# A graph-attention layer in units of half the nodes: two PSUM banks of sums, copied out by ScalarE, and weight tiles of 1024 columns

## The chip, the cores and the metric

The kernel runs on one core of a Trainium2 chip. The metric is the device time of one execution in microseconds (us); less is better. Times of engines below come from one profiled execution.

## The reference

Two layers follow each other, on x of shape (8, 2048, 256) with one adjacency matrix of 2048 by 2048 for all eight batches.

```
# layer 0: attention over chunks of 256 keys, 4 heads of 64
scores = clip(q k^T / 8, -10, 10), -10 where adj == 0
attn   = softmax(scores within each chunk of 256 keys)
x      = layernorm(x + layernorm((sum over chunks of attn v) Wo^T + bo + x))
# layer 1: graph attention, 4 heads of 64
Wh     = x W
e[i,j] = leaky_relu(s_src[i] + s_dst[j], 0.2), -inf where adj == 0
alpha  = softmax(e over j)
x      = layernorm(x + elu(alpha Wh))
```

The exponential of a leaky relu is a maximum of two products, so the kernel forms the weight of layer 1 as max(row factor, column factor) times the adjacency bit; the rest of the column factor is multiplied into Wh once per batch (the tile `waug`, which has a column of ones, times the factor, for the divisor).

## The kernel before

The batches are processed one after the other, and the work of two batches is woven together: while layer 0 of batch b runs, layer 1 of batch b-1 runs beside it. The order of instructions on every engine is the order in which the program lists them; nothing is reordered.

**Layer 0.** A batch has 64 slots (`SLOTS`): 4 groups of 512 queries, 2 pairs of heads, 8 chunks of 256 keys. In slot s the program issues, in this order, the scores of slot s+1 (`scores`, L377 on TensorE, then the masked clip L388 on VectorE), the first head's product of slot s (`product`, L412, copied out of PSUM by ScalarE at L419), the exponentials of slot s+1 (`exps`, L400, ScalarE), one step of layer 1 of the batch before (`lower.step`), and the second head's product of slot s. Around this stand the output projection, the two norms and the projections of layer 1 (`Between`, by tables that name the slot of each step), and the final norm of the batch before that (`Closing`, with tables `CLOSING`, `CLOSING_ALONE` and `ENDING`). Between two batches there is a stretch without slots, written out as the list `order`, in which the next batch is projected.

**Layer 1.** The class `Layer1` works in units: a group of node tiles of 128 (the output rows) and a head. `BANKS = (6, 5, 5)` cuts the 16 node tiles in three groups, so a batch has 12 units, and each unit runs over the 16 tiles of neighbours: 192 tiles in all, `STEP` = 3 in each of the 64 slots. For a tile, `make` forms the weights e on VectorE (L731, 768 or 640 columns), and `use` multiplies them on TensorE (L751), two halves of 64 rows for each node tile, into the unit's sums `pa`, which are held in one PSUM bank (6 x 65 columns of 512). Every such product is two records in the profile. `make` runs `STEP` tiles ahead of `use`. The tiles e live in 4 buffers of the pool `ep`, the adjacency bits `et` in 3 buffers of 4 tiles each (`JG`), loaded two groups ahead, and the row factors `srow` in 2 buffers; all are loaded by SP's queue. The pool `psL` has two banks that its users take in turn: `pa` of layer 1, the mask pieces and one product in the first batch, and one projection per batch.

When a unit is complete, `close` finishes it in pieces, one piece at each later step (`rest`): the divisor and its reciprocal on VectorE (L774, L775, from PSUM), one scaling per node tile on ScalarE from PSUM to `hh` (L779), exponential and relu on ScalarE (L783, L785), and their combination into h1 on VectorE (L787). Meanwhile the next unit writes the other bank of `psL`.

**The ends.** In the last batch `lower.step` is left out of the last `LATE` = 14 slots, and these 14 steps stand in `order` instead, among the steps of the last projection. After it layer 1 of the last batch runs alone, three tiles to a slot, with the final norms of the last two batches beside it.

**The masks.** In the first batch the class `Masks` reads the adjacency in 48 pieces of 128 by 768 or 640, turns them on TensorE and writes clip bounds (`clipD`) and edge bits (`edgeD`, one array for each group of node tiles) to DRAM. The raw pieces `araw` use the pool `ep` as well.

Of the kernel before, what the change touches and what calls it, by code (L numbers as in the profile page):

```python
# [8 lines left out]
F32 = mybir.dt.float32  # L9
# [8 lines left out]
P = 128  # L18
# [4 lines left out]
def adj_resnorm_kernel(  # L23
# [34 lines left out]
    FAR = 100.0  # L58
    BANKS = (6, 5, 5)
    assert D == 64 and KC == HP and 2 * D == P and sum(BANKS) == NT  # L60

# [8 lines left out]
    WIDE = max(BANKS)  # L70
    JG = 4
    assert TILES == STEP * SLOTS and NT % JG == 0

    consts = ctx.enter_context(tc.tile_pool(name="consts", bufs=1))
    big = ctx.enter_context(tc.tile_pool(name="big", bufs=1))
    prp = ctx.enter_context(tc.tile_pool(name="prp", bufs=4))
    ep = ctx.enter_context(tc.tile_pool(name="ep", bufs=4))
    slabs = ctx.enter_context(tc.tile_pool(name="slabs", bufs=4))
    edges = ctx.enter_context(tc.tile_pool(name="edges", bufs=3))
    blocks = ctx.enter_context(tc.tile_pool(name="blocks", bufs=2))  # L80
    small = ctx.enter_context(tc.tile_pool(name="small", bufs=2))
    psA = ctx.enter_context(tc.tile_pool(name="psA", bufs=1, space=bass.MemoryType.PSUM))
    psC = ctx.enter_context(tc.tile_pool(name="psC", bufs=1, space=bass.MemoryType.PSUM))
    psL = ctx.enter_context(tc.tile_pool(name="psL", bufs=2, space=bass.MemoryType.PSUM))
    psM = ctx.enter_context(tc.tile_pool(name="psM", bufs=1, space=bass.MemoryType.PSUM))
# [13 lines left out]

    turn_of = [0]  # L100

    def two_banks(shape, name):

        turn_of[0] ^= 1
        return psA.tile(shape, F32, tag=f"psA{turn_of[0]}", name=name)


# [91 lines left out]
    class Masks:  # L199
# [3 lines left out]
        def __init__(self):  # L203
            self.pieces = [
                (QT * q + u, m) for q in range(NCH) for m in range(len(BANKS)) for u in range(QT)
            ]
            self.raw, self.bits, self.done = [], [], []
            self.next = 0

        def step(self):  # L210
            send()
            if self.next < len(self.pieces):
                t, m = self.pieces[self.next]
                n, j0 = BANKS[m], FIRST[m]
                araw = ep.tile([P, WIDE * P], I32, tag="e", name="araw")
                nc.sync.dma_start(
                    out=araw[:, : n * P], in_=adj[t * P : (t + 1) * P, j0 * P : (j0 + n) * P]
                )
                self.raw.append((t, m, araw))
                self.next += 1  # L220
            if self.bits:
                t, m, ab = self.bits.pop(0)
                self.turn(t, m, ab)
            if len(self.raw) > 2 or (self.raw and self.next == len(self.pieces)):
                t, m, araw = self.raw.pop(0)
                w = BANKS[m] * P
                ab = small.tile([P, WIDE * P], BF16, tag="hh", name="ab")
                nc.vector.tensor_scalar(ab[:, :w], araw[:, :w], 0, None, ALU.not_equal)
                self.bits.append((t, m, ab))
# [4 lines left out]
        def turn(self, t, m, ab):  # L234
            n, j0 = BANKS[m], FIRST[m]
            pm = psL.tile([P, WIDE, P], BF16, tag="psL", name="pm")
            for k in range(n):
                nc.tensor.transpose(pm[:, k, :], ab[:, k * P : (k + 1) * P], identb)
            clip = small.tile([P, WIDE, P], I8, tag="ee", name="clip")
            nc.vector.tensor_scalar(clip[:, :n], pm[:, :n], 2 * CLIP, -CLIP, ALU.mult, ALU.add)  # L240
            edge = small.tile([P, WIDE, P], U8, tag="hp", name="edge")
            nc.scalar.copy(edge[:, :n], pm[:, :n])
            q, u = t // QT, t % QT
            mi = max(k for k in range(len(BANKS)) if FIRST[k] <= t)
            at = (t - FIRST[mi]) * P

            def stores():
                nc.sync.dma_start(
                    out=clipD[q][:, j0 : j0 + n, u * P : (u + 1) * P], in_=clip[:, :n]
                )  # L250
                nc.sync.dma_start(out=edgeD[mi][:, j0 : j0 + n, at : at + P], in_=edge[:, :n])

            outgoing.append(stores)
# [44 lines left out]
    def project(b, g):  # L298
# [14 lines left out]
        def linear(dst, w, bias, apart=False):  # L313
            if apart:
                pps = [psL.tile([P, CH], F32, tag="psL", name="pp") for _ in range(KC)]
            else:
                pp = two_banks([P, KC, CH], "pp")
                pps = [pp[:, c, :] for c in range(KC)]
            for c in range(KC):
                for kc in range(KC):  # L320
                    nc.tensor.matmul(  # L321
                        pps[c],
                        lhsT=w[:, kc, c * P : (c + 1) * P],
                        rhs=st["xT"][:, kc, :],
                        start=(kc == 0),
                        stop=(kc == KC - 1),
                    )
            for c in range(KC):
                nc.scalar.activation(  # L329
                    dst[:, c, cols], pps[c], AF.Identity, bias=bias[:, c : c + 1]  # L330
                )
# [70 lines left out]
    def product(s, k, alone):  # L402
# [3 lines left out]

        pool, tag = (psL, "psL") if alone and k else (psC, "psC")
        pc = pool.tile([P, QT, D1], F32, tag=tag, name="pc")
        for i in range(QT):
# [277 lines left out]
    class Layer1:  # L687
        def __init__(self, b, gd, waug):
            self.b, self.gd, self.waug = b, gd, waug
            self.made = self.used = 0  # L690
            self.rows, self.edge, self.e = {}, {}, {}
            self.tail = []
            self.load_edge(0)
            self.load_edge(1)
            self.load_row(0)
# [22 lines left out]
        def make(self):  # L718
# [8 lines left out]
            if j % JG == 0:  # L727
                self.load_edge(k // JG + 2)
            w = BANKS[m] * P
# [12 lines left out]
        def use(self):  # L742
            k = self.used
            n, j = k // NT, k % NT
            m, h = UNITS[n]
            if j == 0:
                self.pa = psL.tile([P, CH], F32, tag="psL", name="pa")
            e = self.e.pop(k)
            for i in range(BANKS[m]):
                for z in range(2):  # L750
                    nc.tensor.matmul(  # L751
                        self.pa[z * D : (z + 1) * D, i * D1 : (i + 1) * D1],
                        lhsT=e[:, i * P + z * D : i * P + (z + 1) * D],
                        rhs=self.waug[:, j, h, :],
                        start=(j == 0 and i == 0),
                        stop=(j == NT - 1 and i == BANKS[m] - 1),
                        skip_group_check=True,
                    )
            self.used += 1
            if j == NT - 1:  # L760
                self.tail.append(self.close(n, self.pa))

# [4 lines left out]

        def close(self, u, pa):
            m, h = UNITS[u]
            n = BANKS[m]  # L770
            pav = pa[:, : n * D1].rearrange("p (k d) -> p k d", k=n)

            dn = small.tile([P, n, 1], F32, tag="dn", name="dn")
            nc.vector.tensor_scalar(dn, pav[:, :, D:D1], 1e-30, None, ALU.max)  # L774
            nc.vector.reciprocal(dn, dn)  # L775
            yield 1
            hh = small.tile([P, n, D], F32, tag="hh", name="hh")
            for k in range(n):
                nc.scalar.activation(hh[:, k, :], pav[:, k, :D], AF.Copy, scale=dn[:, k, :])  # L779
            yield 1  # L780

            ee = small.tile([P, n, D], F32, tag="ee", name="ee")
            nc.scalar.activation(ee, hh, AF.Exp)  # L783
            hp = small.tile([P, n, D], F32, tag="hp", name="hp")
            nc.scalar.activation(hp, hh, AF.Relu)  # L785
            yield 1
# [58 lines left out]
    for g in range(NCH):  # L845
# [44 lines left out]
    ENDING = {  # L890
        25: [(0, "load")],
        28: [(0, "add")],
        29: [(0, "stats")],
        31: [(0, "finish")],
        46: [(1, "load")],
        49: [(1, "add")],
        50: [(1, "stats")],
        52: [(1, "finish")],
        SLOTS - 1: [(2, "load"), (3, "load")],
# [3 lines left out]
    for b in range(B):  # L903
# [108 lines left out]
        if b + 1 < B:  # L1012
# [3 lines left out]
            order = [begin, *rest, l1, *rest, *first, lambda: before.values((2, 3))]  # L1016
            order += [*rest, ctx, *rest, k0]
            order += [steps[0], t1, steps[1], v0, steps[2], steps[3], l2, k1, steps[4], q0]
# [3 lines left out]
        else:  # L1022
# [4 lines left out]
            order += [steps[7], step, steps[8], step, steps[9], step, fs[0], step, fs[1], step, fs[2]]  # L1027
            order += [step, lambda: lower.rest(4)]
            assert sum(p is step for p in order) == LATE
# [10 lines left out]
    for s in range(SLOTS + 1):  # L1040
        send()
        if s < SLOTS:
            lower.step()
        else:
            lower.rest(4)
        closing.do(s)
# [44 lines left out]
```

## Time and profile before

| What | Value |
|---|---|
| Median of 3 runs | 3788.8 us (3786.09 to 3789.01) |
| The profiled execution | 3787.69 us, of it the span of the instructions 3785.9 us |
| TensorE busy | 3676.4 us, 97% of the span |
| VectorE busy | 3196.2 us, 84% |
| ScalarE busy | 1945.2 us, 51% |
| GpSimd busy | 1385.6 us, 37% |
| Weight tiles e (L731) | 512 of 128x768, mean 1023 ns; 1024 of 128x640, mean 886 ns |
| Layer-1 products (L751) | 32768 records, 1080.3 us busy |
| TensorE's granted clock, mean | 0.992 |

The page gives busy time of each engine, then the span in 40 slices with a digit for the busy tenths, then the groups of instructions with their means and with the idle time of the engine before them. A mean counts an instruction from its first to its last work; back to back, two of them overlap a little, so that the distance from start to start, which the timeline shows, is shorter. The waits name for each idle stretch of an engine what ended it.

### The profile page before, as it was taken

To read this page: it belongs to the slowest core of one execution; us is meant where nothing else is said; L and a number is where in the kernel's file an instruction comes from. 1 tells how busy PE (TensorE), PEld (TensorE's weight loads), DVE (VectorE), ACT (ScalarE), POOL (GpSimd) and SP (SyncE) were. 2 spreads that over 40 slices of the span, in tenths; PEclk is the share of its full clock that TensorE was granted. 3 is DMA by queue.
4 is the path that set the end of the run, shared out by engine and by line. 5 is a ranking of instruction groups with operands and counts; after the bars stand their busy time and mean duration, and the time that the engine had idled before them with its cause. 6 is when DMAs were issued, how large, how long until landed. Compare 5 with 4: busy or idle time off the path is not lost. (4 is left out here: it accounts for less than half of the span.)

```text
span 3785.9 us, 160213 instructions
## 1 busy us (share of the span) xinstructions
PE 3676.4 (97%) x72100; PEld 2747.1 (73%) x72100; DVE 3196.2 (84%) x4810; ACT 1945.2 (51%) x3601; POOL 1385.6 (37%) x1202
## 2 busy tenths in 40 slices
PE   9999999999999999999999999999999999999787
PEld 5656677776777777776777767777677777776676
DVE  5877599987999689995999959998699968998798
ACT  4666445545555555554555545555555555555221
POOL 1445234333434244332433424443344434434310
PEclk9999999999999999999999999999999999999999
DMA  6652334433343343333433434433333334333354
GB/s 163 152 116 69 76 100 105 105 77 113 110 105 100 85 123 102 97 99 85 137 95 94 105 98 125 105 100 81 113 110 102 102 87 123 97 103 81 97 152 120
DMA packets 756545, 398.50 MB, mean 105 GB/s; under 512 B 425744, under 2 KB 721040, under 8 KB 755856
## 3 DMA queue, kind: packets, MB, share of 16 engines
q1 hardware_dynamic: 705856, 354.54, 36.4%
q10 hardware_dynamic: 50000, 33.70, 2.8%
q8 instruction: 564, 9.24, 1.0%
q14 instruction: 125, 1.02, 0.1%
HBM read 331.22 MB, written 56.89 MB: 103 GB/s over the span
## 5 line engine op out<-in xcount | busy, mean ns | idle before, releaser
L388 DVE SCALAR_TENSOR_TENSOR pr<-ps,slab 128x1024 f32<-128x1024 f32 x1024 | 1192.4, 1206 | 197.2 <-PE ps L377 194.4
L731 DVE SCALAR_TENSOR_TENSOR e<-srow,gd,et 128x640 f32<-128x640 f32 (+1 forms) x1536 | 1343.5, 932 | 9.8 <-PE pa L751 5.4
L412 PEld LDWEIGHTS pc<-vaug,pr 128*64 128x64 f32 x32768 | 1039.7, 138 | 408.8 <-issue 308.6
L412 PE MATMUL pc<-vaug,pr 128*64 128x65 f32 x32768 | 1156.3, 224 | 16.2 <-ACT raw L419 9.4
L751 PE MATMUL pa<-waug,e 128*64 128x65 f32 x32768 | 1080.3, 224 | 39.8 <-DVE e L731 38.3
L400 ACT ACTIVATE pr<-pr 128x1024 f32<-128x1024 f32 x1024 | 1044.1, 1056 | 66.8 <-DVE pr L388 55.9
L751 PEld LDWEIGHTS pa<-waug,e 128*64 128x64 f32 x32768 | 1020.5, 139 | 63.9 <-DVE e L731 38.2
L377 PE MATMUL ps<-qT,kT 64*128 64x512 f32 x4096 | 1024.1, 616 | 3.8 <-DVE pr L388 3.1
L419 ACT COPY raw<-pc 128x260 f32<-128x260 f32 x1024 | 384.4, 376 | 1237.5 <-PE pc L412 1206.7
L434 POOL TENSOR_TENSOR part<-raw,rd 128x512 f32<-128x512 f32 x448 | 467.9, 1044 | 1425.4 <-DVE rd L427 1410.9
L436 POOL TENSOR_TENSOR acc<-acc,part 128x512 f32<-128x512 f32 x448 | 575.1, 1284 | 35.2
L377 PEld LDWEIGHTS ps<-qT,kT 64*128 64x128 f32 x4096 | 350.3, 186 | 327.3 <-issue 221.6
L427 DVE RECIPROCAL rd<-raw 128x8 f32<-128x8 f32 x512 | 101.7, 199 | 99.4 <-ACT raw L419 97.5
L434 POOL TENSOR_TENSOR acc<-raw,rd 128x512 f32<-128x512 f32 x64 | 66.7, 1043 | 313.0 <-DVE rd L427 312.2
L779 ACT ACTIVATE hh<-pa,dn 128x64 f32<-128x64 f32 x512 | 114.6, 321 | 101.3 <-DVE dn L775 99.8
L571 PE MATMUL pw<-w_sb,x1T 128*128 128x264 f32 x512 | 139.9, 409 | 5.8 <-DVE x1T L283 4.7
L487 POOL TENSOR_TENSOR rs_c<-rs_c,nhalf 128x4 f32<-128x4 f32 x32 | 55.6, 1737 | 229.3 <-DVE off_c L486 229.3
L527 PE MATMUL po<-wo_sb,qT 128*128 128x256 f32 x512 | 125.5, 390 | 3.1 <-DVE qT L454 2.8
L321 PE MATMUL pp<-xT,wk_sb 128*128 128x512 f32 x256 | 119.3, 610 | 7.9 <-ACT qT L329 6.6
L321 PE MATMUL pp<-xT,wq_sb 128*128 128x512 f32 x256 | 116.2, 597 | 0.0
L337 PE MATMUL pv<-wv_sb,xT 128*128 128x256 f32 x512 | 115.9, 379 | 0.0
L571 PEld LDWEIGHTS pw<-w_sb,x1T 128*128 128x128 f32 x512 | 92.4, 193 | 27.3 <-DVE x1T L283 5.0
(93 smaller groups left out, 1856.5 us busy)
## 6 DMA issues: line engine op xcount, KB each, us to landing
et<-edgeD SPq DMA_DIRECT2D x256, 320.0 KB, 3.1
slab<-clipD SPq DMA_DIRECT2D x512, 128.0 KB, 3.4
et<-edgeD SPq DMA_DIRECT2D x128, 384.0 KB, 3.5
srow<-rowD SPq DMA_DIRECT2D x64, 320.0 KB, 4.2
xg<-in_x_dram SPq DMA_DIRECT2D x32, 512.0 KB, 5.3
x1D<-y ACTq DMA_DIRECT2D x32, 512.0 KB, 4.4
x1g<-x1D SPq DMA_DIRECT2D x32, 512.0 KB, 5.2
out_dram<-o SPq DMA_DIRECT2D x32, 512.0 KB, 3.8
```

Of the source, the lines that this page charges most:

```text
L321: nc.tensor.matmul(pps[c], lhsT=w[:, kc, c * P : (c + 1) * P], rhs=st["xT"][:, kc, :], start=(kc == 0), stop=(kc == KC - 1),)
L377: nc.tensor.matmul(ps[:, k, :], lhsT=kT[rows, hp, t * P : (t + 1) * P], rhs=qT[rows, hp, cols], start=True, stop=True,)
L388: nc.vector.scalar_tensor_tensor(pr, pss[u], -CLIP, slab[:, u, :].unsqueeze(1).to_broadcast([P, 2, CH]), op0=ALU.max, op1=ALU.min,)
L400: nc.scalar.activation(pr, pr, AF.Exp, scale=0.125)
L412: nc.tensor.matmul(pc[z * D : (z + 1) * D, i, :], lhsT=probs[s][u][:, k, i * P + z * D : i * P + (z + 1) * D], rhs=vaug[:, KT * c + u, 2 * ...
L419: nc.scalar.copy(raws[s][:, k], pc)
L434: nc.gpsimd.tensor_mul(part, raw[:, :, :, :D], rd.to_broadcast([P, 2, QT, D]))
L436: nc.gpsimd.tensor_add(accv, accv, part)
L527: nc.tensor.matmul(po[:, k, :], lhsT=qT[:, c, t * P : (t + 1) * P], rhs=wo_sb[:, c, :], start=(c == 0), stop=(c == KC - 1),)
L571: nc.tensor.matmul(pw[:, k, : F + 2 * H], lhsT=self.x1T[:, c, u * P : (u + 1) * P], rhs=w1_sb[:, c, :], start=(c == 0), stop=(c == KC - 1),)
L731: nc.vector.scalar_tensor_tensor(e[:, :w], self.rows[n][:, :w], self.gd[:, h, j : j + 1], self.edge[k // JG][:, j % JG, :w], op0=ALU.max, ...
L751: nc.tensor.matmul(self.pa[z * D : (z + 1) * D, i * D1 : (i + 1) * D1], lhsT=e[:, i * P + z * D : i * P + (z + 1) * D], rhs=self.waug[:, j ...
```

## The change

Layer 1 takes two groups of 8 node tiles (`BANKS = (8, 8)`), so a batch has 8 units and 128 tiles of 1024 columns, two to a slot. A unit's sums fill two banks, which are all of `psL`; when the unit is complete, ScalarE copies both to a tile `sums` in SBUF, in the same step, and `close` works there, in place and in five pieces instead of four. The mask pieces keep their size (`PIECES`). The users of `psL` name their bank in turn (`one_bank`). The pool `ep` has 3 buffers instead of 4; `et` has 4 buffers of 2 tiles instead of 3 of 4, loaded three groups ahead instead of two. The table `ENDING` is moved, since the first two groups of nodes are now complete together.

```diff
-    BANKS = (6, 5, 5)
+    BANKS = (8, 8)
+    PIECES = (6, 5, 5)
...
-    JG = 4
+    JG = 2
+    AHEAD_E = 3
+    n_banks = WIDE // QT
...
-    ep = ctx.enter_context(tc.tile_pool(name="ep", bufs=4))
+    ep = ctx.enter_context(tc.tile_pool(name="ep", bufs=3))
...
-    edges = ctx.enter_context(tc.tile_pool(name="edges", bufs=3))
+    edges = ctx.enter_context(tc.tile_pool(name="edges", bufs=4))
...
-    psL = ctx.enter_context(tc.tile_pool(name="psL", bufs=2, space=bass.MemoryType.PSUM))
+    psL = ctx.enter_context(tc.tile_pool(name="psL", bufs=1, space=bass.MemoryType.PSUM))
...
+    def one_bank(shape, name, kind=F32):
+
+        bank_of[0] ^= 1
+        return psL.tile(shape, kind, tag=f"psL{bank_of[0]}", name=name)
...
             if j == 0:
-                self.pa = psL.tile([P, CH], F32, tag="psL", name="pa")
+                self.pa = [
+                    psL.tile([P, QT, D1], F32, tag=f"psL{i}", name="pa") for i in range(n_banks)
+                ]
...
-                        self.pa[z * D : (z + 1) * D, i * D1 : (i + 1) * D1],
+                        self.pa[i // QT][z * D : (z + 1) * D, i % QT, :],
...
             if j == NT - 1:
-                self.tail.append(self.close(n, self.pa))
+                raw = small.tile([P, WIDE, D1], F32, tag="sums", name="sums", bufs=1)
+                for i, pa in enumerate(self.pa):
+                    nc.scalar.copy(raw[:, i * QT : (i + 1) * QT, :], pa)
+                self.tail.append(self.close(n, raw))
...
-        def close(self, u, pa):
+        def close(self, u, raw):
...
-            nc.vector.tensor_scalar(dn, pav[:, :, D:D1], 1e-30, None, ALU.max)
+            nc.vector.tensor_scalar(dn, raw[:, :, D:D1], 1e-30, None, ALU.max)
             nc.vector.reciprocal(dn, dn)
             yield 1
-            hh = small.tile([P, n, D], F32, tag="hh", name="hh")
             for k in range(n):
-                nc.scalar.activation(hh[:, k, :], pav[:, k, :D], AF.Copy, scale=dn[:, k, :])
+                if k == n // 2:
+                    yield 1
+                v = raw[:, k, :D]
+                nc.scalar.activation(v, v, AF.Copy, scale=dn[:, k, :])
             yield 1
 
             ee = small.tile([P, n, D], F32, tag="ee", name="ee")
-            nc.scalar.activation(ee, hh, AF.Exp)
-            hp = small.tile([P, n, D], F32, tag="hp", name="hp")
-            nc.scalar.activation(hp, hh, AF.Relu)
+            hp = raw[:, :, :D]
+            nc.scalar.activation(ee, hp, AF.Exp)
+            nc.scalar.activation(hp, hp, AF.Relu)
...
-        25: [(0, "load")],
-        28: [(0, "add")],
...
-        46: [(1, "load")],
...
+        35: [(0, "load")],
+        36: [(1, "load")],
+        37: [(0, "add")],
...
-            order += [*rest, ctx, *rest, k0]
+            order += [*rest, ctx, *rest, *rest, k0]
```

## The prediction

> **What bounds the kernel now.** I read the page first, then the time stretched over four windows, then the waits of TensorE in the longest of them, then the timeline of one slot and of the end. The page:
>
> ```profile
> span 3785.9 us, 160213 instructions
> ...
> PE 3676.4 (97%) x72100; PEld 2747.1 (73%) x72100; DVE 3196.2 (84%) x4810; ACT 1945.2 (51%) x3601; POOL 1385.6 (37%) x1202
> ...
> PE   9999999999999999999999999999999999999787
> ...
> DVE  5877599987999689995999959998699968998798
> ```
>
> TensorE is full in every slice but the last three; only there, and in few slices earlier, is VectorE the fuller engine. The windows (busy time of each engine, from the start of layer 1 on):
>
> ```profile
> 450.00:3440.00 2990.00, 2974.69 (x60424) 2245.13 (x60421) 2609.13 (x3896) 1583.34 (x2938) 1155.35 (x992) 1.00 0.39 103
> ...
> 3521.00:3576.00 55.00, 44.37 (x900) 38.94 (x900) 47.21 (x79) 13.83 (x39) 13.55 (x9) 0.92 0.30 81
> 3576.00:3786.00 210.00, 162.75 (x4100) 141.80 (x4096) 195.71 (x319) 43.37 (x127) 22.24 (x19) 0.90 0.47 137
> ```
>
> The columns are the length, then TensorE, its weight loads, VectorE, ScalarE and GpSimd. In the main stretch TensorE idles 15.3 us of 2990; in the last, where only layer 1 of the last batch is left, VectorE is busy 195.7 of 210. The waits of TensorE in the main stretch name no layer-1 tile at all; in the last one they name little else:
>
> ```profile
> PE pp L321 <- ACT qT L329: 5.7, 6, 0.9
> ...
> PE pc L412 <- ACT raw L419: 1.7, 5, 0.5
> ```
> ```profile
> PE pa L751 <- DVE e L731: 30.3, 28, 5.5
> ```
>
> The rate of VectorE there is read from the timeline, start to start: nine weight tiles of 768 columns, then nine of 640, each run followed at once by the next instruction:
>
> ```profile
> 3641.99 8.41 DVE L731 SCALAR_TENSOR_TENSOR e<-srow,gd,et 128x768 f32<-128x768 f32 x9
> 3650.31 0.56 DVE L787 SCALAR_TENSOR_TENSOR h<-ee,hp 128x384 f32<-128x384 f32 x1
> ...
> 3745.11 0.16 DVE L774 TENSOR_SCALAR dn<-pa 128x5 f32<-128x5 f32 x1
> 3745.30 0.19 DVE L775 RECIPROCAL dn<-dn 128x5 f32<-128x5 f32 x1
> 3745.41 7.21 DVE L731 SCALAR_TENSOR_TENSOR e<-srow,gd,et 128x640 f32<-128x640 f32 x9
> 3752.54 0.49 DVE L787 SCALAR_TENSOR_TENSOR h<-ee,hp 128x320 f32<-128x320 f32 x1
> 3752.94 4.86 DVE L731 SCALAR_TENSOR_TENSOR e<-srow,gd,et 128x640 f32<-128x640 f32 x6
> ```
>
> (3650.31-3641.99)/9 is 0.924 us for a tile of 768, (3752.54-3745.41)/9 is 0.792 for one of 640.
>
> [...] 128 columns more cost 0.132 us, so 0.66 of the 0.792 us is columns and 0.13 is fixed. [...] the trace shows the tile e taking up to 2.52 us beside GpSimd's multiply of waug at 3572. [...] the trace shows clock 0.50 after gaps of 2.3 us and more, with 54 matmuls in 2.6 us (48 ns each, waits included) against 82 in 2.2 us (27 ns) later.
>
> **The change part by part.**
>
> *Main stretch.* The layer-1 products are the same 32768 matmul records, one for one. In the slot at 2000 us, 60 of them take from 2000.26 to 2002.01: 29.2 ns each. A slot had 60 or 72 (three tiles of 20 or 24) and will have 64 (two of 32); over a batch the sum is the same. VectorE gains: two tiles at an extrapolated 0.924+2x0.132=1.188 us (2.38) stand for three (2.38 or 2.77), and fewer closings follow. Outside the last part that is worth nothing, since TensorE doesn't wait for VectorE there. ScalarE gains 128 copies of 128x260 at 0.376 us (the row of raw<-pc), 48 us over the run, in an engine at 51%.
>
> The new wait is at a unit's first product: both banks must have been copied out, where before the next unit took the other bank. Units end in slots 7, 15, 23 and so on. After the last product TensorE still has 32 matmuls of layer 0 (0.98), the scores (1.92) and 32 more (1.03): 3.9 us. On ScalarE the slot's two exponentials end some 0.8 us after the unit does (2002.81 against 2002.0), then two copies take 0.7: the banks are free at 1.6. It is covered by 2.3 us. Behind the copies in ScalarE's queue stands the copy of pc (at 2003.43 before), which TensorE needs at 2004.95; it gets later by about 0.1 us. If the cover is gone, each of 56 boundaries costs the excess. Taken: 0.5 us in all; bounds 0 and 5.
>
> Loads: 512 tiles et of 256 KB stand for 384 of 320 or 384 KB, the same bytes; each is still asked for six tiles (7 us) ahead and lands in 3.1 us. The row srow grows to 512 KB (xg, as big, lands in 5.3 us) and is asked for 8 tiles (9.5 us) ahead. At a batch's start srow is waited for; there it comes about 0.3 us later, and the two tiles made take 2.38 instead of 2.77. On SP each et load waits for the tile before on VectorE, as now. Adjacency tiles in three buffers instead of four wait for the conversion one step back, which follows the mask on VectorE that SP awaits anyway. All of these at 0, within 1 us either way.
>
> *Last batch, before 3576.* Its last 14 steps run without layer 0's slots. Before they held 14x60 products, now 14x64: 56x29.2 ns = **1.6 us leave the main stretch** for one where TensorE is busy 44 of 55 us. VectorE has 28x1.188=33.3 us instead of 42x0.792=33.3 of tiles there. Its first tile of a step, made without waiting for this step's products, is larger (1.19 of 2.38 us against 0.79); the products take longer. I take 0, bounds -2 and +2.
>
> *Layer 1 of the last batch alone, with VectorE at its limit.* Tiles: before 64x0.924+128x0.792 = 160.5 us, after 128x1.188 = 152.1. Unit closings: the divisor pair 0.30 and the last step 0.47 or 0.40, before 12x0.30+4x0.47+8x0.40 = 8.7, after 8x(0.30+0.61) = 7.3. Together **-9.8 us**. TensorE needs 32x29.2 = 0.93 us per tile, below 1.19, so VectorE stays the bound. At half clock it needs about 1.74 at twice 27 ns, above 1.19; with three buffers the slack is 2x1.19-1.84 = 0.5 us, so a half-clock stretch of 3.4 us is just swallowed and one of 6.8 is not. Four to five of them: **+1.5**, bounds 0 and 5. Loads of nodes for closing lie at other steps, with the same instructions.
>
> *The two ends of that stretch*, where a unit's closing is on the path:
>
> ```profile
> 3766.50 2.39 PE L751 MATMUL pa<-waug,e 128*64 128x65 f32 x60 [0.40 <-DVE e L731]
> 3768.94 0.17 DVE L774 TENSOR_SCALAR dn<-pa 128x5 f32<-128x5 f32 x1 [0.91 <-PE pa L751]
> 3769.14 0.19 DVE L775 RECIPROCAL dn<-dn 128x5 f32<-128x5 f32 x1
> 3769.43 1.24 ACT L779 ACTIVATE hh<-pa,dn 128x64 f32<-128x64 f32 x5 [9.23 <-DVE dn L775]
> ```
>
> The end grows by 12 products after the last tile (0.35), the second bank's copy with its wait (0.45; the first bank is done half a tile earlier), eight scalings for five (3x0.23[...]: 1.0), exponential and relu of 512 for 320 columns (0.3) and the last step (0.2): **+2.4**. At the start, the last unit of batch 6 closes in the same way, later by some 2.5, but its last step took 1.91 us (3578.69) because GpSimd multiplied waug until 3580.25; later, it takes 0.6: **+1.3**, bounds 0 and 3.
>
> Sum: -9.8-1.6+1.5+2.4+1.3+0.5 = **-5.7 us**. The sum stands against the profiled execution, 3787.69 us (span 3785.9), which lies 1.1 below the median of 3788.8; the difference put on the median gives 3783. About 0.2% (7.6 us) is what a measurement of this kernel can tell from no change.
>
> **The rivals.**
>
> *Boundaries stall (slower).* ScalarE's queue at a unit's end is longer than in the slot I read: the normalisations (y L492, four at 0.59, 2.1 us together) stand in slots 7 or 8 and 11 or 14 of each query chunk. If one comes before the copies, the cover of 2.3 us is used up and, from there on, each further microsecond is TensorE's. At 0.5 us for 56 boundaries: +28-6, **3811 us**. Against it: in program order the normalisation of slot 7 stands behind the copies, and 49% of ScalarE is idle.
>
> *The tail gives more (faster).* No half-clock stall, and the larger first tile shortens the last batch's stage by 2: -5.7-1.5-2.0-0.5 = -9.7, **3779**. For it: VectorE is idle there several times up to 2.1 us for products.
>
> *The tail gives nothing (same).* The 1024-column tile is dearer than the line through two points, or half-clock stretches last longer with three buffers: 128x0.04 = 5 us, or 5 stalls of 1 us: **3788**.
>
> **How the numbers follow.** Forecast 0.57 (its own range 3779.5 to 3787; about a fifth of it lies past -0.2%), more from the tail 0.16, nothing 0.12, stalls 0.15. Faster: 0.16 and 0.18 of the forecast's upper part, 0.34; slower 0.15; within 0.2% 0.51. The range 3777 to 3796 leaves out most of the stalls and a little at the lower end.
>
> **What would show it.** Right: raw-type copies of 128x260 without a TensorE wait on them in the main stretch, its idle time near 15 us; tiles of 1024 at 1.19 us start to start; the stretch from the last GpSimd multiply to the end shorter by 4 to 6 us. Wrong: a row of waits pa <- ACT sums, or pc <- ACT raw, of tens of microseconds; tiles above 1.25; the half-clock share in the last slices grown.

## The result and the profile after

The changed kernel takes **3776.59 us** (3774.41 to 3779.02, 8 runs) against 3788.29 (3786.09 to 3791.16, 8 runs): 11.7 us less, a ratio of 0.9969 with a 95% interval of 0.996 to 0.9977. The forecast was 3783, its range from 3777: the sign was right and the largest part of the gain lies where it was forecast, but the gain is twice what the sum gave. Two executions among all those below ran at a far lower granted clock (4562 and 5636 us, clock 0.76 and 0.60) and are left out. The profiled executions have spans of 3785.9 and 3774.5 us. The page of the kernel after:

```profile
span 3774.5 us, 159666 instructions
...
PE 3664.0 (97%) x72100; PEld 2741.3 (73%) x72100; DVE 3133.7 (83%) x4202; ACT 1988.0 (53%) x3665; POOL 1365.5 (36%) x1202
...
PE   9999999999999999999999999999999999999786
...
DVE  5877489986999689895998959988699977988798
```

VectorE has 62.5 us less to do and ScalarE 42.8 more, but TensorE is still full in every slice but the last three. The time in windows, in the same columns as before (length, TensorE, weight loads, VectorE, ScalarE, GpSimd):

```profile
450.00:3440.00 2990.00, 2976.41 (x60474) 2246.68 (x60474) 2562.34 (x3389) 1617.55 (x2990) 1137.97 (x993) 1.00 0.38 103
...
3576.00:3775.00 199.00, 152.08 (x4096) 135.92 (x4096) 184.64 (x241) 48.54 (x128) 16.80 (x16) 0.91 0.46 138
```

VectorE's work in the last window falls from 195.7 to 184.6 us, and the window ends 11 us earlier. In the main stretch TensorE idles 13.6 us where it idled 15.3. Its waits there:

```profile
PE pp L329 <- ACT qT L337: 5.7, 6, 0.9
PE pc L422 <- ACT pr L408: 2.9, 6, 0.5
PE pt L470 <- POOL acc L446: 2.7, 6, 0.4
PE pt L300 <- ACT y L502: 2.0, 12, 0.2
```

No wait for a unit's two copies appears, so the boundary costs nothing; and the row of pc waiting for ScalarE's raw copy, 1.7 us in five waits before, is gone. One period of the lone part of layer 1, in the timeline:

```profile
3650.47 0.16 DVE L788 TENSOR_SCALAR dn<-sums 128x8 f32<-128x8 f32 x1
3650.66 0.20 DVE L789 RECIPROCAL dn<-dn 128x8 f32<-128x8 f32 x1
3650.78 9.61 DVE L741 SCALAR_TENSOR_TENSOR e<-srow,gd,et 128x1024 f32<-128x1024 f32 x8
3660.31 0.69 DVE L803 SCALAR_TENSOR_TENSOR h<-ee,sums 128x512 f32<-128x512 f32 x1
```

Start to start, (3660.31-3650.78)/8 is 1.191 us for a tile; 1.188 had been extrapolated.

To see where the time went I cut both traces at the same pieces of work. The marks are the start of the last stretch in which layer 0 still works without slots (its first transposes of the contexts); the first product of the last batch's own layer 1, which follows the last batch's copy of its factors, `flat`; the end of the last layer-1 product; and the end:

| Part | before | after | change | forecast |
|---|---|---|---|---|
| Up to the last stretch with layer 0 | 3525.6 | 3521.1 | -4.5 | -1.1 |
| That stretch and the start of the lone part | 56.1 | 56.7 | +0.6 | +1.3 |
| Layer 1 alone | 187.2 | 177.8 | -9.4 | -8.0 |
| After the last product | 17.0 | 18.9 | +1.9 | +2.1 |
| Sum | 3785.9 | 3774.5 | -11.4 | -5.7 |

The forecast column puts the prediction's terms in these parts: +0.5 and -1.6; 0 and +1.3; -9.8, +1.5 and 0.35; the rest of +2.4. The 0.35 us are the 12 products that the forecast counted to the end of the kernel; they stand before the last product's end.

### The profile page after: what moved, and what is told of

It reads as the page before. It is cut to its first block, busy times and chain, and to the rows that moved or that the text cites. A ratio compares the mean times of both kernels' runs of the same rounds, so it can differ in the third digit from the quotient of the medians.

```text
span 3774.5 us, 159666 instructions
## 1 busy us (share of the span) xinstructions
PE 3664.0 (97%) x72100; PEld 2741.3 (73%) x72100; DVE 3133.7 (83%) x4202; ACT 1988.0 (53%) x3665; POOL 1365.5 (36%) x1202
## 4 chain that ended last, share of the span: by engine, by line
PE 86%; DVE 5%; issue 3%; ACT 3%; DMA 1%; POOL 1%; SPq 0%; ACTq 0%; DVEq 0%; POOLq 0%
PE pc L422 26%; PE ps L385 24%; PE pa L763 22%; PE pp L329 5%; PE po L537 3%; PE pw L581 3%; PE pv L345 2%; DVE e L741 2%; ACT y L502 1%; DVE pr L396 1%; ACT pr L408 1%; DMA xp<-in_x_dram 0%; PE pm L246 0%; ACT qT L337 0%; SPq L279 0%
## 5 line engine op out<-in xcount | busy, mean ns | idle before, releaser
L741 DVE SCALAR_TENSOR_TENSOR e<-srow,gd,et 128x1024 f32<-128x1024 f32 x1024 | 1273.1, 1286 | 10.4 <-PE pa L763 5.8
L795 ACT ACTIVATE sums<-sums,dn 128x64 f32<-128x64 f32 x512 | 134.0, 337 | 9.7 <-DVE dn L789 9.3
```

The costliest lines, as they stand in the source:

```text
L741: nc.vector.scalar_tensor_tensor(e[:, :w], self.rows[n][:, :w], self.gd[:, h, j : j + 1], self.edge[k // JG][:, j % JG, :w], op0=ALU.max, ...
```

## The experiments

Twelve kernels ran, each in five rounds beside the kernel before on the same chip; ratios are to it. The theory **A** is that the main stretch gained because VectorE is nearly full in the early slots of a batch, so that TensorE there did wait, through ScalarE, for VectorE. The rival **B** is that it is ScalarE's own queue, eased by the finer pieces of a unit's end. Kernels whose first batch is the same reach batch 1 between 434 and 438 us: so much of a span is scatter, and I compare the parts. Batches 1 to 6 are steadier: the ten kernels, after among them, that have the same program there take 2697.8 to 2699.4 us.

**The order of the group sizes alone.** The kernel before, with the wide group in the second place:

```diff
-    BANKS = (6, 5, 5)
+    BANKS = (5, 6, 5)
```

> The kernel before with BANKS = (5, 6, 5): the same computation, but the 768-column tiles stand in slots 21 to 42 of a batch, where no final norm runs on VectorE, instead of slots 0 to 21, where one does. Theory A (the 3.4 us that the main stretch gained unforeseen are short stalls of TensorE where VectorE was nearly full, with 768-column tiles and a final norm in the same slots): TensorE's waits pc <- ACT raw between 450 and 3440 us go from 1.7 us to near 0, the last inter-batch stretch (transposes of the context, at 3525.6 us before and 3521.1 after the change) starts 2 to 3.5 us earlier than 3525.6, and the whole is 2 to 3.5 us faster than before. Theory B (the gain is of the edit's other parts: ScalarE's closings in smaller pieces and from SBUF, the loads of et in smaller tiles): no difference from before, within 1 us.

Measured: 3786.27 us, ratio 0.9993 (0.9984 to 1.0001), which as a whole can't be told from none. The trace can: batches 1 to 6 take 2698.4 us (before 2700.4, after 2698.1) and batch 7's slots 388.5 (389.2 and 387.0, of which 1.6 are the moved products). The same 120 us early in a batch, in the windows of before, after and this kernel in turn:

```profile
900.00:1020.00 120.00, 119.66 (x2842) 94.24 (x2842) 117.71 (x173) 66.62 (x119) 52.93 (x45) 1.00 0.43 126
```
```profile
900.00:1020.00 120.00, 120.00 (x2744) 93.06 (x2746) 113.28 (x154) 68.04 (x120) 51.88 (x46) 1.00 0.42 123
```
```profile
900.00:1020.00 120.00, 120.00 (x2740) 93.00 (x2740) 115.32 (x180) 67.15 (x119) 53.48 (x47) 1.00 0.45 124
```

VectorE, the third of the busy times, was at 117.7 of 120 us before; at 115.3 TensorE, the first, has no gap left. The wait of pc for raw is not in this kernel's trace either. In the trace before, it stands as follows (slot 13 of batch 2, slots counted from 0; lines of other work are left out):

```profile
971.62 2.87 DVE L731 SCALAR_TENSOR_TENSOR e<-srow,gd,et 128x768 f32<-128x768 f32 x3
...
974.52 2.31 DVE L388 SCALAR_TENSOR_TENSOR pr<-ps,slab 128x1024 f32<-128x1024 f32 x2
...
975.73 2.19 ACT L400 ACTIVATE pr<-pr 128x1024 f32<-128x1024 f32 x2 [1.49 <-DVE pr L388]
...
977.82 0.51 ACT L783 ACTIVATE ee<-hh 128x384 f32<-128x384 f32 x1
978.24 0.51 ACT L785 ACTIVATE hp<-hh 128x384 f32<-128x384 f32 x1
978.65 0.35 ACT L419 COPY raw<-pc 128x260 f32<-128x260 f32 x1
...
979.05 1.15 PE L412 MATMUL pc<-vaug,pr 128*64 128x65 f32 x32 [0.34 <-ACT raw L419]
```

VectorE goes from three weight tiles straight to the masked clip; ScalarE waits 1.49 us for it, then takes the exponentials and two pieces of a unit's end before it copies pc.

Slot by slot, once the different number of products is taken off, the kernel before loses 0.41, 0.40, 0.47, 0.75, 0.41 and 0.79 us against after in the first 22 slots of batches 2 to 7, 3.2 in all, and nothing in batch 1, which has the wide tiles but no final norm. This kernel loses at most 0.13 in any of them. In batches 2, 3, 6 and 7 most of the loss is the wait shown, before the first product of slot 14. In batches 4 and 5 it is one gap earlier, in slots 4 and 1; that these have the same origin is not shown. So the main stretch is shorter, beyond the moved products, by 2.7 us here and by 2.9 after, and here with nothing but another order of the group sizes. That order also makes ScalarE's pieces in these slots smaller (exponential and relu take 0.46 us each for 320 columns, 0.51 for 384), so this run alone does not tell the two engines apart.

**VectorE loaded again.** The kernel after, with one reduction of 128x256 (0.404 us) on VectorE in each of the first 22 slots of a batch:

```diff
-                    lower.step()
+                    lower.step(s < 22)
...
+            if padded:
+                nc.vector.tensor_reduce(pad, gamma_sb, AX.X, ALU.max)
```

> The changed kernel with one more VectorE instruction (a reduction of 128x256[...]) in each of slots 0 to 21 of batches 1 to 7, which brings VectorE's load there back to about that of before (2.77 us of tiles a slot instead of 2.38); layer 1 alone at the end is untouched. Theory A: the stalls of TensorE come back, and the run is 2 to 4 us slower than the changed kernel (3778.5 to 3780.5). Theory B: the same as the changed kernel, within 1 us.

Measured: 3785.35 us, ratio 0.9991 (0.9984 to 0.9997), 8.8 more than after; batches 1 to 6 take 2705.3 us, 7.2 more than after. The wait is back, in the main stretch's waits of TensorE:

```profile
PE pc L423 <- ACT raw L430: 3.8, 6, 0.6
```

The loss is the same in each of batches 2 to 6: 0.95 us before slot 10 and 0.49 before slot 14, the place of the wait before. Batch 1, which has the added reductions but no final norm, loses nothing. A dose on VectorE alone brings the stall back, and more of it than expected, so A is shown as a cause. The waits above name only a part of the loss; ahead of slot 10 the products of layer 1 also take longer, 2.28 us for 64 instead of 2.04. The mean load alone does not decide: in the window from 900 to 1020 us VectorE is busy for less time than before (117.7), yet TensorE has a larger gap.

```profile
900.00:1020.00 120.00, 119.28 (x2724) 92.60 (x2722) 116.52 (x172) 68.74 (x120) 49.55 (x46) 1.00 0.41 121
```

**ScalarE's pieces.** The kernel after, with the eight scalings of a unit in one piece:

```diff
-                if k == n // 2:
-                    yield 1
```

> The changed kernel with all eight scalings of a unit in one piece of the closing, as before (then five or six), so that ScalarE has 2.0 us in one slot instead of 1.0 in two. Theory A: no difference from the changed kernel, within 1 us. Theory B: 2 to 4 us slower, with waits of TensorE for ScalarE in the main stretch.

Measured: 3778.87 us, ratio 0.9974 (0.9963 to 0.9984), 2.3 more than after, as B expected. Batches 1 to 6 take 2.3 us more than after, and the wait returns, at a third of its size in the run before this:

```profile
PE pc L422 <- ACT raw L429: 1.1, 6, 0.2
```

It stands once in each of batches 2 to 7, before the first product of slot 10, and lengthens each by 0.25 us, 1.5 in all. A expected nothing here, so A alone is not enough: the stall lies at the end of a chain, from VectorE's masked clip over ScalarE's exponentials and its pieces of a unit's end to its copy of pc, and either engine can lengthen it. The rest is single gaps that I could not assign.

**Fewer steps moved.** The kernel after, with four of the 14 steps of the last batch back in its slots:

```diff
-    LATE = 14
+    LATE = 10
```

> The changed kernel with LATE = 10 instead of 14: four of the last batch's steps go back from the last inter-batch stretch to the slots (those that stood before the adding of y, the norm's application, the transposes and the first half of the values). By the sum's price of a moved step the main stretch gets 4 x 1.87 us of products, less the 0.53 us that TensorE waits for ScalarE in each slot without a step: +5.4 us. Theory C (in the last stretch TensorE's order puts each step's products ahead of the chain, so that each of these steps delays it by about 1.9 us): -7.6 us there, in all 2 us faster than the changed kernel. Theory D (these steps lie in the shadow of VectorE's and ScalarE's chain, as the forecast had it): nothing gained there, in all 5 us slower.

Measured: 3777.46 us, ratio 0.9969 (0.9958 to 0.9981). In the traces the slots grow by 4.5 us and the last stretch shrinks by 2.4. A step thus costs 1.1 us in the slots and saves 0.6 in the stretch, between the two theories: a step in the stretch is neither free nor as dear as its products. The four steps should cost 2.1 us in all; the median is 0.9 higher than after. So the number 14 was not made wrong by the change.

**The start of the lone part: order.** The last step of batch 6's last unit after the first two tiles of batch 7:

```diff
-            order += [step, lambda: lower.rest(5)]
+            order += [step, lambda: lower.rest(4)]
+            last = lower
...
+    last.rest(1)
```

> The changed kernel, but at the start of the last part (layer 1 of the last batch alone) VectorE makes its first two weight tiles before it takes the last step of batch 6's last closing. In the changed kernel VectorE waits 3.5 us there for ScalarE's relu and then takes 2.4 us for that step beside GpSimd, and the first product starts at 3577.8 us. If this start is bound by VectorE's order, the first tile can start once srow has landed (asked for at 3569.2, 5.0 us), about 3574.3 instead of 3576.4: 1 to 2.5 us faster than the changed kernel. If it is bound by srow or by GpSimd's multiply of waug (until 3575.9, which the product needs), at most 0.5 us faster.

Measured: 3776.11 us, ratio 0.9964 (0.9951 to 0.9977), the same as after. The first product follows `flat` 2.5 us sooner, but the lone part is 2.3 longer (180.1). The timeline shows what the tiles paid, first merged, then one by one, from narrow windows, with GpSimd's multiplies of waug:

```profile
3573.41 4.77 DVE L741 SCALAR_TENSOR_TENSOR e<-srow,gd,et 128x1024 f32<-128x1024 f32 x2 [2.62 <-DMA srow<-rowD]
```
```profile
3572.33 1.91 POOL L688 TENSOR_TENSOR waug<-waug,ed 128x1024 f32<-128x1024 f32 x1
3573.41 1.90 DVE L741 SCALAR_TENSOR_TENSOR e<-srow,gd,et 128x1024 f32<-128x1024 f32 x1 [2.62 <-DMA srow<-rowD]
3574.20 2.90 POOL L688 TENSOR_TENSOR waug<-waug,ed 128x1024 f32<-128x1024 f32 x1
3575.24 2.94 DVE L741 SCALAR_TENSOR_TENSOR e<-srow,gd,et 128x1024 f32<-128x1024 f32 x1
```

Two tiles take 4.77 us where two take 2.4 elsewhere, and the ends of the two engines' instructions alternate. The first tile ends 1.1 us after the multiply that was running (at 3574.24), the next multiply 1.8 after that tile (at 3575.32), the second tile 1.1 after that multiply (at 3577.10); alone, a tile takes 1.28 and a multiply 1.9. Of the tiles and the unit's last step, what VectorE runs first pays: the tiles here, the last step in the changed kernel (2.39 us, here 0.68).

**The start: without GpSimd.** The same order, and the last batch's multiply moved from GpSimd to VectorE, two heads ahead of the divisor pair and two behind it:

```diff
-            for h in range(H):
-                nc.gpsimd.tensor_mul(
+            if b < B - 1:
+                scaled(range(H), nc.gpsimd)
...
-            order += [step, lambda: lower.rest(5)]
+            order += [step, lambda: fs[3](0, 1), lambda: lower.rest(1), lambda: fs[3](2, 3)]
+            order += [lambda: lower.rest(3)]
```

> The changed kernel with only the start of the lone stretch altered: the last batch's multiply by the divisors on VectorE in two halves, and the first two tiles ahead of the last closing step. Contention with GpSimd as the cause: from the ScalarE copy of the transposes to the first product 8.5 us or less (10.7 after, 8.2 in e5) with the lone part back at about 178 us (180.1 in e5), so 1 to 2.5 us less than after. Rival: VectorE is only loaded more; then within 0.5 us of after or up to 2 slower.

Measured: 3772.75 us, ratio 0.9959 (0.9945 to 0.9972), 3.8 us less than after. Timelines of after and of this kernel:

```profile
3567.43 8.51 POOL L688 TENSOR_TENSOR waug<-waug,ed 128x1024 f32<-128x1024 f32 x4
...
3574.09 2.39 DVE L803 SCALAR_TENSOR_TENSOR h<-ee,sums 128x512 f32<-128x512 f32 x1 [3.47 <-ACT sums L801]
```
```profile
3566.71 2.35 DVE L681 TENSOR_TENSOR waug<-waug,ed 128x1024 f32<-128x1024 f32 x2
...
3573.40 2.82 PE L767 MATMUL pa<-waug,e 128*64 128x65 f32 x48 [5.41 <-DVE e L745]
3574.37 0.69 DVE L807 SCALAR_TENSOR_TENSOR h<-ee,sums 128x512 f32<-128x512 f32 x1
```

The last step of the unit takes 0.69 instead of 2.39 us, the first product follows `flat` by 8.1 us instead of 10.7, and the lone part stays at 178.4, so 2.1 us are kept between `flat` and the last product, where the order alone kept 0.3. Contention was the cause. The rest lies earlier and is not shown to be of this edit: 1.2 us in the stretch before `flat`, where the two other kernels with the same program (e12_all, e14_combined) take as long as after, and 0.5 in the slots and the first batch.

**The table of the end.** The kernel after, with the second node group of the last batch closed at slots 46 to 52 again:

```diff
-        36: [(1, "load")],
...
+        46: [(1, "load")],
+        49: [(1, "add")],
```

> The changed kernel with the closing of the last batch's second group of nodes back at its old steps (load 46, add 49, stats 50, finish 52); the first group stays at 35 to 40. This undoes a part of the moved table ENDING. Theory E (the 178 us of layer 1 alone are VectorE's sum of durations, wherever a closing stands): the same as the changed kernel within 0.5 us in that part. Rival: two closings close together keep TensorE idle longer or colder than two apart, and then this is 1 to 2 us faster or slower.

Measured: 3776.68 us, ratio 0.9965 (0.9953 to 0.9978), the lone part 178.5 us against 177.8. Three other kernels with the lone part of after (e2_pad, e3_one_piece, e6_late10) take 178.0 to 178.5 there, so where the closings lie makes no difference that can be measured: VectorE has the same work.

**VectorE relieved in the lone part.** In the lone part six final norms take their sums on VectorE (bn_stats, 24 of 410 ns, and bn_aggr, 24 of 150 ns). Here ScalarE forms them, with the accumulating output of its activations:

```diff
+                for i, f in enumerate((AF.Identity, AF.Square)):
+                    nc.scalar.activation(
+                        junk, self.src[:, k, :], f, accum_out=self.mv[:, k, i : i + 1]
+                    )
```

> The changed kernel with the sums for six of the final norms (all four of batch 6 and the first two of batch 7) taken by ScalarE, as sums of x and of its squares, instead of by VectorE's bn_stats and bn_aggr; VectorE keeps four small instructions. In the part where layer 1 runs alone, a closing's statistics take VectorE 1.93 us (3587.34 to 3589.27) and then about 0.45. Theory E: VectorE bounds that part, so it shortens by 6 x 1.5 = 9 us less what TensorE's half-clock stretches take, 7 to 9 us, and the run is at 3768 to 3770. Rival (TensorE's clock or its products bound it nearly as much, since they are at 76% there): 0 to 3 us.

Measured: 3771.52 us, ratio 0.995 (0.9937 to 0.9963); the lone part 173.6 us, 4.2 less than after instead of the 7 to 9 expected. The lone part's windows, of after and of this kernel:

```profile
3578.00:3756.00 178.00, 151.91 (x4096) 135.72 (x4095) 175.37 (x214) 41.09 (x110) 13.48 (x12) 0.95 0.49 147
```
```profile
3578.00:3752.00 174.00, 147.94 (x4096) 132.27 (x4096) 167.99 (x179) 64.79 (x206) 12.65 (x12) 0.98 0.50 151
```

VectorE's 175.4 busy us of 178 fall to 168.0 of 174, so 7.4 us of work went and about 3 of them came back as waits. VectorE's longest wait of this part, and a new one of TensorE, name ScalarE:

```profile
DVE h L822 <- ACT sums L820: 2.6, 1, 2.6
PE pa L782 <- ACT sums L794: 2.4, 2, 1.3
```

That VectorE sets this part is shown: relieved, it is shorter, and moving the work within it (the table of the end) does nothing.

**The two together.** ScalarE's sums and the tiles ahead of the last closing step:

```diff
...
-            order += [step, lambda: lower.rest(5)]
+            order += [step, lambda: lower.rest(4)]
```

> Both: the first two tiles made first and the sums on ScalarE. If they add, 8 to 11 us faster than the changed kernel, 3766 to 3768.

Measured: 3770.8 us, ratio 0.9949 (0.9936 to 0.9962), within 1 us of the sums alone and above the 3766 to 3768 expected. With GpSimd still multiplying, the order brings nothing here either.

**ScalarE's sums at other steps.** One closing to a unit's period, away from the unit's end. In this kernel and the next, batch 6's second node group is added to only after the first unit's end has written one head of batch 7 over it, so 64 columns of one node group of batch 6's output are those of batch 7. The last kernel below has the right order.

```diff
-        2: [(0, "sums"), (1, "add")],
-        3: [(1, "sums")],
+        1: [(0, "add"), (0, "sums")],
...
+        10: [(1, "add")],
+        11: [(1, "sums")],
```

> In the changed kernel's layer 1 alone VectorE is the engine that never stops (175.4 us busy in 3578 to 3756). This kernel gives the six norms' eight sums to ScalarE, as e9_sums_act did, and also places the closing steps in the middle of a unit's period, so that ScalarE's sums (eight of about 0.55 us) don't lie where a unit's scaling waits for ScalarE's copy. If e9's gain was cut to 4.2 us by those collisions, the lone stretch is 169 to 171 us (against 177.8 after, 173.6 in e9) and the whole 3766 to 3770. Rival: the new waits come from the order of VectorE's own queue whatever the places are; then it is as e9, 173 to 174 and about 3771.5.

Measured: 3771.77 us, ratio 0.9954 (0.9941 to 0.9966), the lone part 173.1: no gain over the first places. The rival was right in the number, but the cause it named is not shown. The waits of VectorE are again for ScalarE: 2.0 us in which the first unit's last step waits for ScalarE's reading of the group that it overwrites, which is new, and four of 0.34 for copies of sums that stand behind ScalarE's normalisations.

**Sums apart, and no GpSimd at the start.**

> e11_sums_apart, and at the start of the last batch's lone stretch the multiply by the divisors is on VectorE in two halves instead of one long GpSimd instruction, and the first two tiles are made before the last closing step. If it is GpSimd's access beside VectorE's that makes the first h and tiles take 2.4 us instead of 0.7 and 1.2, this gains a further 1 to 2.5 us. Rival: the first unit waits for another input (the divisors' reciprocals, the copy of the transposes), then 0.5 or less, or a loss of the 1 to 2 us that VectorE spends on the multiply.

Measured: 3768.31 us, ratio 0.9945 (0.9933 to 0.9958); the first product 8.1 us after `flat`, the lone part 173.2. From `flat` to the last product this is 2.5 us less than with the sums apart alone, so the start's gain adds to that of the sums.

**All that gained.** The last kernel, with the second group closed before the first unit's end:

```diff
-        10: [(1, "add")],
-        11: [(1, "sums")],
-        13: [(1, "moments")],
+        2: [(1, "add"), (1, "sums")],
...
+        4: [(0, "finish"), (1, "moments")],
```

> The pieces that gained, together: e12_all, with the closing of batch 6's second node group back ahead of the first unit's end (in e11_sums_apart and e12_all its addition came after that unit's end had written the first head of batch 7 over it, so that 64 columns of one node group of batch 6's output were those of batch 7). If the start of the lone stretch (2.5 us) and the sums on ScalarE (4.2 us) add up, it is 3767 to 3770, as e12_all; if the wait of the first unit's end for ScalarE's sums (2.0 us in e11_sums_apart and e12_all) goes with the move, up to 2 less. Rival: the sums of two groups close together hold the first unit's scaling again, then 3770 to 3772 as e10_act_first.

Measured: **3766.35 us**, ratio 0.9939 (0.9926 to 0.9953), 10.2 us less than after. From `flat` to the last product it takes 178.3 us where after takes 188.5: the whole difference. Its wait for the read of the overwritten group is gone, as expected, and the lone part is 2.5 us shorter than in the kernel before it (170.7), somewhat more than that wait. What is left there, in VectorE's and TensorE's waits:

```profile
DVE dn L811 <- ACT sums L798: 2.7, 4, 1.7
```
```profile
PE pa L786 <- ACT sums L798: 4.9, 4, 1.3
```

TensorE's four waits, and three of VectorE's four (0.34 us each), are for copies of a unit's sums that stand behind other work in ScalarE's queue: three times behind the normalisations `o`, once (TensorE alone) behind the sums for a norm. It is the boundary wait which the changed kernel itself does not have. VectorE's fourth, 1.7 us, is at the end of the last unit and is there in the changed kernel too.

## Why the prediction was wrong, point by point

**The step that failed** is "Outside the last part that is worth nothing, since TensorE doesn't wait for VectorE there", with its term "Taken: 0.5 us in all; bounds 0 and 5". It bounded the main stretch by a loss only. The part came out at -4.5 us against -1.1. Of the 4.5, 1.6 are the products moved, as predicted (batch 7's slots fall by 2.2). The other 2.9 are short stalls of TensorE in the first 22 slots of batches 2 to 7, 0.40 to 0.79 us in each, where 768-column tiles and a final norm lay together on VectorE; in two of the six batches the gap stands elsewhere, and its origin is open. The loss of 0.5 that the forecast had put there did not come. The row "PE pc L412 <- ACT raw L419: 1.7, 5, 0.5" stood in the prediction's own fence. I read it as ScalarE's, since that is the engine it names, and missed that the copy was late because ScalarE had been waiting for VectorE; the slot that the prediction read, at 2000 us, lies in the second half of a batch, where no final norm runs. ScalarE's own pieces stand in that chain too, so neither engine alone is the cause. This one step is 3.4 of the 5.7 us by which the sum was short.

**Layer 1 alone**, forecast -8.0 (-9.8, +1.5 and 0.35 of products), was -9.4. The tile was right (1.191 for 1.188 us). The term that was mis-sized is the half-clock stretches, "+1.5, bounds 0 and 5". The lengths it used are those of the trace before, where the granted clock is 0.50 for 6.8 us from 3598.2 and from 3622.2, and for 3.4 from 3683.6 and from 3738.2. After, they are there (granted clock 0.84 to 0.91 in three of nine windows of this part, all with closings in them; 0.95 in the mean, 0.94 before), but VectorE's wait for TensorE, which is how they would cost anything, is 0.2 us in all, so three buffers are enough here. That is the 1.4 us of this part's miss. From the last GpSimd multiply to the end the kernel is 7.1 us shorter (198.6 for 205.7), where the forecast had 4 to 6.

**The end** was +1.9 for +2.1. As the forecast had it, ScalarE's copies begin (3755.19) while TensorE still writes the second bank (until 3755.61). Of the 1.0 us that it gave the scalings, the 0.3 beyond "3x0.23" were not shown by any trace; measured, a scaling takes 337 ns from SBUF and took 321 from PSUM, 16 ns that make 0.13 us for eight. Exponential and relu grew by about 0.5 instead of 0.3.

**The start**, with the stretch before it, was +0.6 for +1.3, and not for the reason given: the stretch up to `flat` grew by 0.6, for which the forecast had 0, and from `flat` to the first product it takes 10.7 us in both kernels. "Later, it takes 0.6" failed: the last step still met GpSimd's multiply and took 2.39 us. Nor was the closing later: the last step began 7.0 us after `flat` (3574.09-3567.1), before it 7.7 (3578.69-3571.0). Before, the third tile of batch 6's last step met the multiply (three tiles took 4.15 us, and TensorE waited for it until 3574.78); after, the second and last tile was already running when the multiply began. The forecast counted the closing and not these tiles.

**The rivals.** The boundary stalls did not come: no wait of TensorE on the two copies, in any of the windows. The case in which the tail gives more reached 3779 by a half-clock term of 0, which was right, by a shorter last stage, which was not (it is 0.6 longer), and by no loss in the main stretch; it had no gain there. The case in which the tail gives nothing needed a dearer tile or longer half-clock stretches; neither came. That is why the measured time lies just below the range: a gain for the main stretch had been given no bound at all, though its own fence showed a wait there of 1.7 us, and VectorE was 98% busy in a part of it.

## What to carry to other kernels

When a wait names a fast engine's copy, follow the copy's own wait one step further back before calling the engine ahead of it idle; here a mean of 87% busy over 3 ms hid 98% over 120 us, and even the mean over 120 us did not tell how much was lost. Give every stretch a bound on both sides, also where the path's engine looks full. Where one engine sets a stretch, take instructions off it rather than move them about, and look at what the receiving engine has in its queue at the moments when the others wait for it.

## What the runs showed of the hardware that was not expected

- Beside GpSimd's multiply of waug, VectorE's tile e and combination h took longer, and so did the multiply. After the change, h took 2.39 us instead of 0.69, 1.70 more, where the multiply that was running had 1.85 left (until 3575.94). In e5_make_first, the first tile took 0.62 more with 0.83 of a multiply left, the next multiply 0.98 more with 1.11 of that tile left, and the second tile 1.66 more with 1.86 of that multiply left. So the price in these four was nearly the rest of the other's instruction, and not a fixed factor. The reciprocal of dn took its usual 0.20 beside a multiply (at 3570.42). The multiply of four heads takes 8.51 us on GpSimd, its first head, begun beside a running tile, 2.88 instead of 1.92; on VectorE it takes 4.7.
- The 48 activations with an accumulating output in the lone part of e9_sums_act (417 ns in the mean for 128x256) come with 48 more instructions that read the accumulator, 186 ns each.
- A granted clock of 0.84 from 3680 to 3700 us, after the change, cost nothing there, as VectorE was busy 19.75 of the 20.
